# Attention block, v by two levels of block products: the other orientation, two turns, and inner sums kept in DRAM

## The chip, the cores and the metric

The kernel runs on one core of one Trainium2 chip. The metric is the device time of one execution in microseconds (us). Everything is fp32.

## The reference

For 16 images x of 512 channels by 32 x 32 pixels (n = 1024), the block computes group normalisation, one 512 to 1536 projection, attention in 4 heads of 128 channels, an output projection and a residual:

```
xn = (x - mu_group) * rsqrt(var_group + 1e-5) * gamma + beta      # 8 groups
q, k, v = split(qkv_w @ xn + qkv_b)                               # 512 x 1024 each
attn = softmax(q^T k / sqrt(128))                                 # per head, 1024 x 1024
out = x + proj_w @ (attn applied to v) + proj_b
```

## The kernel before

**Layout.** An image is four tiles `x` of 128 channels by 1024 pixels. A head is eight steps. Each step computes scores for 128 keys against two halves of 512 queries (`s`, L609), takes their exponential on ScalarE (`p`, L614), adds `p` into the running denominators `tot` on VectorE (L620, L622), and multiplies the `p` of the step before by v (`po`, L694). The stationary operand of L694 is a block of v laid out as [m, d]: 128 pixels on the partitions, 128 channels of the head in the free dimension.

**Block products.** The projections use seven products in place of eight for a 2 x 2 block product (`strassen`, in the order 1, 2, 6, 5, 7, 4, 3, with two accumulators `x` and `y` in PSUM). A unit is one of the seven products with its eviction: ScalarE copies (`kept_copy`, L399, and L484), VectorE adds (L486, L570). q/k and the output projection use two levels of it (`two_levels`): seven outer products in four groups `OUTER`, each of seven inner ones, so 49 products of 128 x 128 weights with 256 columns in all. For the inner level VectorE makes four sums of the outer operand (`inner_sum`, L460), in single-buffered tiles `in_t1` to `in_t4`. `combine` adds the groups, and `finish` writes the result. q/k is done in two pairs of heads, and both pairs make the same inner sums of the same image. v uses one level only (`v_units`): weights move and x is stationary, so that v comes out as [m, d] directly. That is two times seven products of four 256-column matmuls, 56 per image, evicted by L568 and L570.

**Order.** `plan_head` spreads the units of other stages over the eight steps of each head. For image b: head 0 carries q/k pair 1 of image b, head 1 the projection of image b-1 together with the load and statistics of image b+1, head 2 v of image b+1, head 3 q/k pair 0 of image b+1. Statistics are `bn_stats` and `bn_aggr` on VectorE (L40, L41); normalisation is an activation on ScalarE (L82). The sums of x for the outer level (`x_sums`, L255) stand at the start of head 2. From this program a scheduler makes the order of each engine's instructions, which each engine then follows in turn. DMAs are issued by SP's queue, also in turn: weights from DRAM (L331, v's L541), residual and output (L581, L594), and for the denominators a row written to DRAM and read back broadcast (L641, L643), which the division L704 waits for.

**Buffers.** Two weight tiles (`w`), four tiles of x, three of v, three of `p`, four `y`, two PSUM banks for scores, and two each for `x` and `y`.

Of the kernel before, what the change touches and what calls it, by code (L numbers as in the profile page):

```python
# [27 lines left out]
class Norm:  # L28
# [49 lines left out]
    def apply(self, xn, x, sc, sh, c, on_scalar):  # L78

        i = slice(c, c + 1)  # L80
        if on_scalar:
            self.nc.scalar.activation(xn, x, AF.Identity, bias=sh[:, i], scale=sc[:, i])  # L82
        else:
            self.nc.vector.tensor_scalar(xn, x, sc[:, i], sh[:, i], ALU.mult, ALU.add)
# [69 lines left out]
def fast_path(ctx, tc, x, sources, out, consts, flag, dims):  # L154
# [4 lines left out]

    nc = tc.nc  # L160
# [60 lines left out]
    def stats_chunk(b, c):  # L221
        if c == 0:
            mvs[b] = gn.tile([P, NCC, 2], F32, tag="mv", name=f"mv_{b}")
        norm.chunk(mvs[b], xs[b, c], c)
# [5 lines left out]
    def normalise(b, c, half):  # L230
        t = xs[b, c][:, ts(half, HALF)]
        sc, sh = scaled[b]

        norm.apply(t, t, sc, sh, c, b > 0 or c % 2 == 1)
# [37 lines left out]
    def raw_blocks(site):  # L272


        if site == "proj":
            first, second = proj_wT[:, 0:HC], proj_wT[:, HC:C]
        else:
            first = qkv_wT[:, site * Q : (site + 1) * Q]
            second = qkv_wT[:, C + site * Q : C + (site + 1) * Q]
        return {  # L280
            "a11": first[: C // 2, :], "a12": first[C // 2 :, :],
            "a21": second[: C // 2, :], "a22": second[C // 2 :, :],
        }
# [10 lines left out]
    for site in (*range(PAIRS), "proj"):  # L294
# [4 lines left out]
    store["v"] = kept.tile([P, 7, KC, HC], F32, name="kept_v")  # L299
# [3 lines left out]
    def stage_blocks(site):  # L303
# [4 lines left out]
        if site == "proj":  # L308
# [70 lines left out]
    def v_sums():  # L379
        nc.vector.tensor_sub(wv["s2"], wv["s1"], wv["a11"])  # L380
        nc.vector.tensor_sub(wv["s3"], wv["a11"], wv["a21"])
        nc.vector.tensor_sub(wv["s4"], wv["a12"], wv["s2"])
        for i, p in enumerate(ORDER):
            nc.sync.dma_start(store["v"][:, i], wv[FACTORS[p][0]])
# [50 lines left out]
    def two_levels(name, site, b, blocks, finish):  # L435


        R = {}

# [4 lines left out]
        def group_units(g):  # L444
            group = OUTER[g]
            n = len(group)
            have = {}

            def weights():
                R[g] = rpool.tile([P, 2, 2, HALF], F32, tag=f"r{g % 3}", name=f"{name}_r{g}")  # L450
                have["w"] = group_weights(site, g, b == 0 and site != "proj")

            def inner_sum(m):
                have[m] = tpool.tile([P, 2, Q], F32, tag=f"in_{m}", name=f"{name}_{g}_{m}")
# [4 lines left out]
                for i in range(n):  # L459
                    nc.vector.tensor_sub(have[m][:, i, :], inner(i, a), inner(i, c))  # L460

# [14 lines left out]
            def out_(which, a, c=None):  # L476
# [16 lines left out]
                p5, p7, p4, lambda: (p3(), combine(g)),  # L493
            ]

# [12 lines left out]

        return [group_units(g) for g in range(len(OUTER))]

    def qk_groups(b, pair):
# [14 lines left out]
        return two_levels(f"qk_{b}_{pair}", pair, b, lambda: xb[b], finish)  # L526

    def v_units(b, jj):


        w = {}

        def weights(i):
            if b == 0:
                return wv[FACTORS[i][0]]
            at = ORDER.index(i)
            if at % 3 == 0:
                n = min(3, 7 - at)
                t = wpool.tile([P, 2 * 7 * P], F32, tag="w", name=f"w_v_{b}_{jj}_{at}")
                t = t[:, : n * KC * HC].rearrange("p (i k m) -> p i k m", k=KC, m=HC)  # L540
                nc.sync.dma_start(t, store["v"][:, at : at + n])  # L541
                for j in range(n):
                    w[ORDER[at + j]] = t[:, j]
            return w[i]

        def mm(acc, i, first):
            wi, bn = weights(i), FACTORS[i][1]
# [24 lines left out]
        return strassen(f"v_{b}_{jj}", mm, out_)  # L572

# [115 lines left out]
    def weighted_sum(s, half):  # L689
        b, h, j = where(s)  # L690
        if j == 0 and half == 0:
# [3 lines left out]
            po[b, h][:, i], vs[b, h // 2][:, h % 2, j, :], ps[s][:, i],  # L695
# [29 lines left out]
    def kept_projection():  # L725
        stage_sums("proj")
        for g in range(len(OUTER)):
            group_weights("proj", g, True)
# [106 lines left out]
    def plan_head(b, h):  # L835

        plan = [[] for _ in range(NB)]
        if h == 0:
            spread(plan, staggered(qk_groups(b, 1)), 0, NB)
            if b > 0:  # L840
                plan[3].append(lambda: o_blocks(b - 1))
                plan[3].append(lambda: sums_of_b(ob[b - 1]))
        elif h == 1:
            if b == 0:
                plan[0].append(lambda: stage_blocks("proj"))
                spread(plan, [lambda o=o: bias_of_v(o) for o in range(NCC)], 2, 6)
                plan[6].append(kept_projection)
            else:
                spread(plan, staggered(proj_groups(b - 1)), 0, NB)
            if b + 1 == B:  # L850
                plan[0].append(lambda: last_loads("x"))
            else:
                plan[0].append(lambda: load_x(b + 1))
                spread(plan, [lambda c=c: stats_chunk(b + 1, c) for c in range(NCC)], 2, 6)
                plan[5].append(lambda: stats_group(b + 1))
                plan[6] += [
                    lambda c=c, half=half: normalise(b + 1, c, half)
                    for half in range(NH2) for c in range(NCC)
                ]
# [9 lines left out]
        elif b + 1 < B:  # L869
            if h == 2:  # L870
                plan[0].append(lambda: x_sums(b + 1))
                spread(plan, staggered([v_units(b + 1, jj) for jj in range(2)]), 1, NB)
            else:
                spread(plan, staggered(qk_groups(b + 1, 0)), 0, NB)
# [20 lines left out]
    for half in range(NH2):  # L895
        for c in range(NCC):
            normalise(0, c, half)
    with tc.issue_after(before_power.ins):
        nc.vector.tensor_add(wv["s1"], wv["a21"], wv["a22"])
    v_sums()  # L900
    x_sums(0)
    run(staggered([v_units(0, 0), v_units(0, 1)]))
    stage_sums(0)
    run(staggered(qk_groups(0, 0)))
    stage_blocks(1)
# [3 lines left out]
    for s in range(steps + 1):  # L909
        units = []  # L910
        if s < steps:
# [3 lines left out]
            units = plan[j]  # L915
        if 0 < s < steps and s % NB == 0:
# [146 lines left out]
```

## Time and profile before

| | |
|---|---|
| time, 3 runs | 3233.07 us median (3231.42 to 3233.31) |
| profiled span | 3230.6 us |
| PE busy | 3204.0 us, 99%, 10684 matmul records |
| DVE (VectorE) busy | 2453.7 us, 76% |
| ACT (ScalarE) busy | 1246.6 us, 39% |
| DMA | 357.32 MB, mean 111 GB/s |
| repeat of one image in the chain of waits | 199.2 us |

An fp32 product is two matmul records, and each has a weight load of its own (PEld), which overlaps the matmul before it. A record's duration is longer than the distance to the next one, since matmuls are pipelined; so PE's throughput is read from the distance between starts. A timeline line gives start, duration, engine, source line, operation, output and inputs, and the number of merged records. In the table of windows each line is one stretch of time: its length, then the busy time of PE, PEld, DVE, ACT and POOL, then the granted clock, the DMA share and GB/s.

### The profile page before, as it was taken

To read this page: it belongs to the slowest core of one execution; us is meant where nothing else is said; L and a number is where in the kernel's file an instruction comes from. 1 tells how busy PE (TensorE), PEld (TensorE's weight loads), DVE (VectorE), ACT (ScalarE), POOL (GpSimd) and SP (SyncE) were. 2 spreads that over 40 slices of the span, in tenths; PEclk is the share of its full clock that TensorE was granted. 3 is DMA by queue.
4 is the path that set the end of the run, shared out by engine and by line. 5 is a ranking of instruction groups with operands and counts; after the bars stand their busy time and mean duration, and the time that the engine had idled before them with its cause. 6 is when DMAs were issued, how large, how long until landed. Compare 5 with 4: busy or idle time off the path is not lost.

```text
span 3230.6 us, 31083 instructions
## 1 busy us (share of the span) xinstructions
PE 3204.0 (99%) x10684; PEld 2009.2 (62%) x10684; DVE 2453.7 (76%) x4392; ACT 1246.6 (39%) x2169; POOL 17.6 (1%) x22
## 2 busy tenths in 40 slices
PE   7999999999999999999999999999999999999999
PEld 6566666666666666666666666666666666666654
DVE  7859689586885868868688686877859778596784
ACT  2433334343343333433334333343343334343442
POOL 0000000000000000000000000000000000000000
PEclk9999999999999999999999999999999999999999
DMA  5423333233232333323333333323323333233331
GB/s 171 154 79 126 109 108 125 84 115 120 96 135 74 126 116 104 120 92 116 108 108 120 103 112 109 114 104 107 122 94 115 114 114 117 87 115 109 114 128 40
DMA packets 114837, 357.32 MB, mean 111 GB/s; under 512 B 15472, under 2 KB 27248, under 8 KB 114672
## 3 DMA queue, kind: packets, MB, share of 16 engines
q1 hardware_dynamic: 112800, 353.15, 31.6%
q10 hardware_dynamic: 1872, 2.11, 0.2%
q8 instruction: 86, 1.41, 0.2%
q14 instruction: 79, 0.65, 0.1%
HBM read 308.10 MB, written 47.12 MB: 110 GB/s over the span
## 4 chain that ended last, share of the span: by engine, by line
PE 92%; DVE 6%; ACT 1%; issue 1%; POOL 1%; DMA 0%; SPq 0%; DVEq 0%; POOLq 0%
PE s L609 25%; PE po L694 25%; PE qk_x L471 12%; PE qk_y L471 9%; PE v_x L550 7%; PE v_y L550 5%; PE pp_x L471 5%; PE pp_y L471 4%; DVE tot L622 2%; DVE y L590 1%; DVE y L593 1%; DVE pp_r L503 1%; POOL rstd L64 1%; PE lx L777 0%; DVE pp_r L486 0%
## 5 line engine op out<-in xcount | busy, mean ns | idle before, releaser
L609 PE MATMUL s<-qk,qk 128*128 128x512 f32 x2048 | 1049.0, 594 | 1.8 <-DVE qk L521 1.3
L694 PE MATMUL po<-p,v 128*128 128x512 f32 x2048 | 1045.4, 593 | 0.7 <-ACT p L614 0.7
L614 ACT ACTIVATE p<-s 128x512 f32<-128x512 f32 x1024 | 611.1, 597 | 1065.3 <-PE s L609 1028.1
L622 DVE TENSOR_TENSOR tot<-tot,p 128x1024 f32<-128x1024 f32 x385 | 469.2, 1219 | 313.7 <-ACT p L614 310.7
L694 PEld LDWEIGHTS po<-p,v 128*128 128x128 f32 x2048 | 387.1, 190 | 442.6 <-issue 416.6
L609 PEld LDWEIGHTS s<-qk,qk 128*128 128x128 f32 x2048 | 386.3, 190 | 112.2 <-issue 54.8
L471 PEld LDWEIGHTS qk_x<-qk_t,w 128*128 128x128 f32 x1344 | 250.5, 190 | 200.4 <-issue 139.7
L471 PE MATMUL qk_x<-qk_t,w 128*128 128x256 f32 x1344 | 358.1, 383 | 1.7 <-ACT qk_u L399 1.4
L399 ACT COPY qk_u<-qk_x 128x512 f32<-128x512 f32 (+1 forms) x256 | 136.4, 533 | 238.6 <-PE qk_x L471 238.6
L486 DVE TENSOR_TENSOR qk_r<-qk_y,qk_u 128x512 f32<-128x512 f32 (+1 forms) x256 | 158.7, 620 | 23.5 <-PE qk_y L471 21.2
L550 PE MATMUL v_y<-w_v,x 128*128 128x256 f32 x720 | 173.1, 380 | 0.1
L550 PEld LDWEIGHTS v_x<-w_v,xt 128*128 128x128 f32 x720 | 136.8, 190 | 57.0 <-issue 43.0
L550 PE MATMUL v_x<-w_v,xt 128*128 128x256 f32 x720 | 170.1, 379 | 0.0
L550 PEld LDWEIGHTS v_y<-w_v,x 128*128 128x128 f32 x720 | 135.6, 190 | 55.1 <-issue 40.7
L471 PE MATMUL pp_x<-pp_t,w_proj 128*128 128x256 f32 x630 | 167.8, 383 | 0.0
L471 PEld LDWEIGHTS pp_x<-pp_t,w_proj 128*128 128x128 f32 x630 | 117.2, 190 | 73.7 <-issue 44.5
L471 PE MATMUL qk_y<-x,w 128*128 128x256 f32 x512 | 141.8, 379 | 0.0
L521 DVE SCALAR_TENSOR_TENSOR qk<-qk_r,qkb_sb,qk_r 128x512 f32<-128x512 f32 x192 | 135.5, 746 | 1.5 <-ACT qk_r L484 0.4
L570 DVE TENSOR_TENSOR v<-v_y,v_u 128x512 f32<-128x512 f32 x64 | 43.7, 683 | 116.2 <-ACT v_u L399 71.8
L399 ACT COPY pp_u<-pp_x 128x512 f32<-128x512 f32 (+1 forms) x120 | 63.9, 532 | 161.1 <-PE pp_x L471 150.3
L486 DVE TENSOR_TENSOR qk_r<-qk_y,qk_p 128x512 f32<-128x512 f32 (+1 forms) x128 | 79.2, 618 | 57.3 <-PE qk_y L471 57.3
L471 PEld LDWEIGHTS qk_y<-x,w 128*128 128x128 f32 x512 | 97.3, 190 | 39.7 <-issue 22.0
(174 smaller groups left out, 3445.8 us busy)
## 6 DMA issues: line engine op xcount, KB each, us to landing
w<-kept SPq DMA_DIRECT2D x90, 896.0 KB, 4.5
w_v<-kept_v SPq DMA_DIRECT2D x60, 768.0 KB, 4.2
w_proj<-kept_proj SPq DMA_DIRECT2D x45, 896.0 KB, 4.7
rinv<-row SPq DMA_DIRECT2D x63, 512.0 KB, 3.6
out_y<-y SPq DMA_DIRECT2D x124, 256.0 KB, 2.2
x<-in_x SPq DMA_DIRECT2D x60, 512.0 KB, 4.1
y<-in_x SPq DMA_DIRECT2D x120, 256.0 KB, 3.8
w<-kept SPq DMA_DIRECT2D x30, 448.0 KB, 3.3
```

What stands on the lines that cost most here:

```text
L64: nc.gpsimd.tensor_tensor(rstd, ve, self.neghalf, ALU.pow)
L399: nc.scalar.copy(t[n][:, :width], t["x"][:, :width])
L471: nc.tensor.matmul(acc[:, ts(i, Q)], have["w"][:, i, SLOTS[an], :], inner(i, bn), start=(first and i == 0), stop=True, skip_group_check=True,)
L486: nc.vector.tensor_add(dst, view(a), view(c))
L503: nc.vector.tensor_add(part(2, 0), part(1, 1), part(2, 0))
L521: nc.vector.scalar_tensor_tensor(st[b, h][:, ts(half, HALF)], a[:, r, :], qkb_sb[:, i : i + 1], c[:, r, :], ALU.add, ALU.add,)
L550: nc.tensor.matmul(acc[:, ts(g, HC)], xb[b][bn][k][:, ts(2 * jj + g, P)], wi[:, k, :], start=(first and g == 0 and k == 0), stop=(k == KC ...
L570: nc.vector.tensor_add(dst, view(a), view(c))
L609: nc.tensor.matmul(sc, ks[b, h][:, ts(j, P)], qs[b, h][:, ts(half, HALF)], start=True, stop=True)
L614: nc.scalar.activation(ps[s][:, ts(half, HALF)], sc, AF.Exp, scale=SCALE)
L622: nc.vector.tensor_add(tot[b, h][:, i], tot[b, h][:, i], ps[s][:, i])
L694: nc.tensor.matmul(po[b, h][:, i], vs[b, h // 2][:, h % 2, j, :], ps[s][:, i], start=(j == 0), stop=(j == NB - 1),)
```

## The change

**v.** For images 1 to 15, v goes through `two_levels` like q/k: weights stationary, x moving, 49 products of 256 columns. It comes out as [d, m]. `finish` (in `v_groups`) adds two parts, turns 32 x 32 blocks on VectorE into an interleaved layout, writes 128 x 512 to DRAM (`vd`) and reads it back in four pieces of 32 partitions into v, whose layout is now such that a 128 x 128 block has four floats between neighbouring elements of its free dimension. Image 0 keeps the old v.

**Inner sums.** q/k pair 0 makes the inner sums and also writes them to DRAM (`sums="keep"`); v and q/k pair 1 load them instead of making them (`sums="load"`), each tile one group ahead, the first group's at the last step of the head before.

**Order.** Head 2 now carries q/k pair 0 of the next image and head 3 its v. Statistics of images 1 to 15 move to ScalarE (two passes with an accumulated sum, and three small scalings); normalisation and the sums of x move to steps 5 to 7 of head 1. In image 0, v's weights are combined and kept in head 1, and the first x sums stand after the last VectorE normalisation.

```
-        norm.chunk(mvs[b], xs[b, c], c)
+        if b == 0:
+            norm.chunk(mvs[b], xs[b, c], c)
+            return
+
+        junk = lpool.tile([P, N], F32, tag="tt", name=f"junk_{b}_{c}")
+        sums = gn.tile([P, 3], F32, tag="st", name=f"sums_{b}_{c}")
+        nc.scalar.activation(junk, xs[b, c], AF.Identity, accum_out=sums[:, 0:1])
+        nc.scalar.mul(mvs[b][:, c, 0:1], sums[:, 0:1], 1.0 / N)
+        nc.scalar.mul(sums[:, 1:2], sums[:, 0:1], -1.0 / N)
+        nc.scalar.activation(
+            junk, xs[b, c], AF.Square, bias=sums[:, 1:2], accum_out=sums[:, 2:3]
+        )
+        nc.scalar.mul(mvs[b][:, c, 1:2], sums[:, 2:3], 1.0 / N)
...
+            def sum_tile(h, m):
+                haves[h][m] = tpool.tile(
+                    [P, 2, Q], F32, tag=f"in_{m}", name=f"{name}_{h}_{m}"
+                )
+                return haves[h][m][:, : len(OUTER[h])]
+
+            def load(h, m):
+                if sums == "load" and h < len(OUTER):
+                    nc.sync.dma_start(sum_tile(h, m), inner_kept[b, h, m])
...
+                if sums == "keep":
+                    t = dpool.tile([P, n, Q], F32, tag=f"{m}_{g}", bufs=1, name=f"kept_{m}_{g}")
+                    inner_kept[b, g, m] = t
+                    nc.sync.dma_start(t, have[m][:, :n])
...
-                p5, p7, p4, lambda: (p3(), combine(g)),
+                lambda: (load(g + 1, "t2"), p5()), lambda: (load(g + 1, "t1"), p7()),
+                lambda: (load(g + 1, "t3"), p4()),
+                lambda: (load(g + 1, "t4"), p3(), combine(g)),
...
+    def v_groups(b):
+
+        def finish(which, a, c):
...
+            n = P // BLK
+            for h in range(2):
+                t = ypool.tile([P, HALF], F32, tag="y", name=f"vt_{b}_{pair}_{h}_{half}")
+                nc.vector.tensor_add(t, a[:, h, :], c[:, h, :])
+
+                u = ypool.tile([P, HALF], F32, tag="y", name=f"vu_{b}_{pair}_{h}_{half}")
+                nc.vector.transpose(
+                    u.rearrange("p (q i j) -> p j q i", q=n, i=BLK),
+                    t.rearrange("p (j q i) -> p j q i", q=n, i=BLK),
+                )
+                row = dpool.tile([P, HALF], F32, tag="v", name=f"vd_{b}_{pair}_{h}_{half}")
+                nc.sync.dma_start(row, u)
+                for q in range(n):
+                    nc.sync.dma_start(
+                        vs[b, pair][ts(q, BLK), h, half].rearrange("m (k i) j -> m k (i j)", k=n),
+                        row.rearrange("(k m) (q e) -> q m k e", m=BLK, q=n)[q],
+                    )
...
+    def v_block(b, h, j):
+        v, n = vs[b, h // 2][:, h % 2], NB // NH2
+        return v[:, j, :] if b == 0 else v[:, j // n, :, j % n]
...
-                spread(plan, staggered([v_units(b + 1, jj) for jj in range(2)]), 1, NB)
-            else:
-                spread(plan, staggered(qk_groups(b + 1, 0)), 0, NB)
+        elif h == 2:
+            spread(plan, staggered(qk_groups(b + 1, 0)), 0, NB)
+        else:
+            spread(plan, staggered(next_v.pop()), 0, NB)
```

## The prediction

> **What bounds the kernel now.** I read the page's busy line first, then the costliest groups, then the timeline in a quiet stretch, then the windows of one image.
>
> ```profile
> PE 3204.0 (99%) x10684; PEld 2009.2 (62%) x10684; DVE 2453.7 (76%) x4392; ACT 1246.6 (39%) x2169; POOL 17.6 (1%) x22
> ...
> L609 PE MATMUL s<-qk,qk 128*128 128x512 f32 x2048 | 1049.0, 594 | 1.8 <-DVE qk L521 1.3
> L694 PE MATMUL po<-p,v 128*128 128x512 f32 x2048 | 1045.4, 593 | 0.7 <-ACT p L614 0.7
> ...
> L694 PEld LDWEIGHTS po<-p,v 128*128 128x128 f32 x2048 | 387.1, 190 | 442.6 <-issue 416.6
> ...
> L550 PE MATMUL v_y<-w_v,x 128*128 128x256 f32 x720 | 173.1, 380 | 0.1
> ```
>
> PE is busy 99% of the span and its groups wait for next to nothing. A busy PE need not be at its peak, so the timeline of PE must give the real price of a product (each fp32 product is two records, "x2"):
>
> ```profile
> 575.62 1.02 PE L694 MATMUL po<-p,v 128*128 128x512 f32 x2
> 576.47 1.89 PE L550 MATMUL v_x<-w_v,xt 128*128 128x256 f32 x8
> 578.20 1.02 PE L609 MATMUL s<-qk,qk 128*128 128x512 f32 x2
> 579.06 1.02 PE L694 MATMUL po<-p,v 128*128 128x512 f32 x2
> ```
>
> Start to start, a 512-column product takes 0.858 us (578.20 to 579.06) and four 256-column products 1.73 us, so 0.432 each. One image, from the built order of PE: 64 scores and 64 weighted sums of 512 columns (128 x 0.858 = 109.8), and 203 products of 256 columns (q/k 98, projection 49, v 56; 203 x 0.432 = 87.7): 197.5 us. The chain of waits repeats every 199.2 us (for example "PE po" at 759.00, 958.22, 1157.44). So only 1.7 us per image is not peak matmul, small statistics products included. Columns can be saved, waits hardly.
>
> The second view is the windows of one image; the columns are PE, PEld, DVE, ACT, POOL, then clock and DMA share:
>
> ```profile
> 494.00:504.00 10.00, 10.00 (x33) 5.89 (x31) 10.00 (x19) 4.57 (x9) 0.00 (x0) 1.00 0.43 159
> ...
> 554.00:564.00 10.00, 10.00 (x33) 5.58 (x32) 9.85 (x23) 6.59 (x12) 0.00 (x0) 1.00 0.35 135
> 564.00:574.00 10.00, 10.00 (x36) 6.56 (x35) 6.62 (x12) 2.96 (x5) 0.00 (x0) 1.00 0.22 79
> 574.00:584.00 10.00, 10.00 (x36) 6.54 (x35) 2.15 (x3) 2.96 (x5) 0.00 (x0) 1.00 0.10 26
> ```
>
> DVE is full around the projection and nearly idle in the v stage behind it. That idle time is the reserve from which DVE catches up.
>
> **What the Trainium skill says.** TensorE: Matmul & The Clock Gate, step-by-step part: weights of the next product are loaded under the current one. The trace agrees: the 190 ns load of the weighted sum ends in an "issue" gap of 0.24 us. SBUF — State Buffer, the note on cachelines under Door 1: fp32 reads 16 bytes apart touch a new line each and pay a penalty, without a figure. No row here shows such a load. ScalarE: Activation LUTs, What ACT_TABLE_LOAD costs: 186 ns + 0.833 ns per column, 93 ns more per pointer operand. The trace agrees (L82, two pointers, 512 columns: 799; L763, one pointer, 1024: 1150). DMA: Bandwidth & Descriptors, Two DMAs through the same engine are not ordered: a read of what a DMA wrote must wait for its completion; the row/rinv pair already does (1.3 us, then 3.6 us to landing).
>
> **The change, part by part, per image of 15 (image 0 keeps the old v).**
>
> *PE.* v falls from 56 to 49 products of 256 columns: 7 x 0.432 = 3.02 us, times 15 = 45.4 us. This is the only part that acts directly on the path.
>
> *PE weights.* v now lies in SBUF with 4 floats between neighbours, so each weighted sum loads strided weights. Lower bound 190 ns (no penalty). If reading takes twice as long, 128 columns go from about 107 to 213 ns above the same fixed part: about 297 ns, an estimate from the 190 and the page. Behind a 512-column pass of 429 ns that is hidden; behind a 256-column pass (215 ns) it shows 82 ns. The built order has about 14 such places per image, up from 8: 1.1 us. Upper bound at four times, about 510 ns: 81 ns on both passes of all 64, 10 us. I take 0.5 us.
>
> *DVE.* Removed: 8 bn_stats and 4 aggregates (8 x 0.669 + 4 x 0.197 = 6.1), 28 inner sums of q/k pair 1 now loaded (28 x 0.415 = 11.6), 6 v evictions (6 x 0.682 = 4.1): 21.8 us. Added: 12 evictions at 0.62 (7.4), three 1024-wide combinations at 1.22 (3.7), 8 adds at 0.685 (5.5), 8 transposes of 512. No row shows these: half of L629's 1240 ns plus its fixed part gives 0.70, with strided writes at most double, 1.4; at 0.70 it is 5.6. Sum 22.2. So DVE's total is unchanged (+0.4, up to +6). Only its place changes.
>
> *ACT.* Removed 8 copies at 0.584 (4.7). Added 16 copies at 0.532 (8.5) and the statistics, by the page's price 1.04 + 1.13 + 3 x 0.19 = 2.7 per chunk, 11.0 in all. 78 us becomes 93 of some 197; hidden in sum, but the statistics lie as one block of about 17 us (with exponentials and copies between) in the projection, and DVE's mean copy (L47) waits for its end.
>
> *DMA and SP.* 46 DMAs and 21.7 MB per image become 132 and 36.5 MB: 8 row writes and 32 reads of 64 KB for v, 16 writes and 32 loads of inner sums, 4 instead of 6 v weight loads. Issues at about 0.33 us: 44 us of SP, of 197. 36.5 MB in 197 us is 185 GB/s; the first 20 us of the trace moved 270. SP waits for each row write (1.3 us for 4 KB, 2.2 for the 256 KB of out_y); behind it in the queue stand the first weights of q/k pair 1 and the rinv load. PE's pair-1 products and DVE's division wait for those. In the built order PE has 15 score/weighted-sum pairs (25.7 us) between v's last product and pair 1's first, so this wait is covered; v's own second half is needed about 17 us after its last product against some 12 (eviction 0.7, adds and transposes 2.8, write 2.2, issues 2.6, landing 3 to 4).
>
> *Where it comes back.* The built order pushes pair 1 of q/k into one clump: 49 products with only 8 of 512 columns between, 28.0 us, and then the projection, 47.3 us. DVE work placed there, summed by the rows and scaled by 0.91 (the same sum for the kernel before gives 167.8 us per image where DVE is busy 152.6): 25.2 and 50.2 us. So 75.4 us of DVE stand against 75.3 of PE. In the old order this pair had 95.1 against 98.1. Within the clump each block's c22 eviction (copy 0.53, add 0.62) sits between its p7 and its p3, with 0.86 to 1.7 us of PE work between; at the clump's end the projection's first inner sums queue behind q/k finishes and the denominators. I count 2 us of stall there and 1 us in the projection beyond today's: bounds 0 and 8, as the q/k stage that follows (DVE 35.5 of 49.1) can absorb a lag. But 1.7 of today's total already holds such waits, so I add 1.3 net of them. With the weights: 3.0 - 0.5 - 1.3 = 1.2 us kept per image, 18 us.
>
> *Start and tail.* DVE is full from 60 to 140 us (19.2, 18.2, 19.7, 17.2 of 20). 28 sums leave it, 16 kept writes and the keeping of v's weights (some 11 us of DVE, in head 1, where DVE is busy 5.75 of 20) come: -3 us, between -8 and +4. The last projection is unchanged.
>
> Sum against the profiled span: 3230.6 - 18 - 3 = 3209.6; runs lie 1 to 3 us above that span, so 3211.
>
> **Rivals.** (1) *Full gain*: the order was laid out so that loads and DVE just arrive; 45.4 + 3: about 3185. For it: today only 1.7 us per image is lost although DVE is full in places. (2) *Nothing left*: 3.0 us of stalls per image, 3233. (3) *Slower: DVE becomes the bound from the q/k clump through the projection.* Around the projection DVE was busy about 52 of 57 us, 91%, waiting for PE and ACT in turn; at 91%, 75.4 us take 82.9, which is 7.6 beyond PE, less 3.0 saved and less the part of today's 1.7 that lies there: up to +4 per image, 60 us; half of that absorbed gives 3262. It decides from 3.0 us of added stall, which is DVE at 96% of that stretch. Against it: a full window of 10.00 exists and stalls can be made up later. (4) *Strided weights at a quarter of the rate*: 10 us per image, 150 - 48: about 3335. Against it: a penalty of that size must be in the memory, and the page gives none. (5) *It does not do what it says*: excluded by the built order, which has the 49 products.
>
> **How the numbers follow.** Forecast (1 to 2.5 us kept, 3192 to 3222) 0.42; full gain 0.22; nothing left 0.11; DVE-bound 0.19; strided weights 0.06. Faster 0.42 + 0.22 = 0.64, same 0.11, slower 0.25; 0.2% (6.5 us) is about what a measurement of this kernel can tell from no change. The range leaves out a twentieth below 3182 and, above 3255, the strided weights and the worse part of the DVE case.
>
> **What would show it.** Matmul records about 210 fewer; DVE busy near 2450; weights of po at 190 to 300 ns; PE idle for DVE or ACT in the clump and at the projection's first sums; repeat near 198.0. Wrong if po's weights exceed 430 ns, if PE waits for w or t loads by more than 1 us per image, or if the repeat is over 199.2.

## The result, and the profile after

The changed kernel takes 3281.01 us (median of 4 runs, 3278.69 to 3282.86) against 3232.57 us before: a ratio of 1.015, with a 95% interval of 1.0132 to 1.0167. It is slower by 48 us. The profiled spans are 3281.0 and 3230.6 us.

The busy line and the DMA line of the page, and two of its groups (line, engine, operation, count, then busy us and mean ns of one):

```profile
PE 3203.2 (98%) x10474; PEld 2157.9 (66%) x10474; DVE 2509.4 (76%) x4161; ACT 1444.5 (44%) x2709; POOL 23.1 (1%) x22
...
DMA packets 308600, 589.30 MB, mean 180 GB/s; under 512 B 36800, under 2 KB 137664, under 8 KB 308416
...
L755 PEld LDWEIGHTS po<-p,v 128*128 128x128 f32 x2048 | 597.0, 303 | 320.9 <-issue 190.1
...
L617 DVE STREAM_TRANSPOSE vu<-vt 128x512 f32<-128x512 f32 x120 | 134.8, 1123 | 1.5
```

There are 210 matmul records fewer, as the change says, so 45.4 us of products are gone. PE is busy for almost as long as before all the same. The time came back as idle time, and the view of waits of PE says behind what (us in total, times, longest); the first three rows have no counterpart in the kernel before, whose longest row, "pm" apart, is shown below them:

```profile
PE qk_x L501 <- DMA w<-kept: 16.5, 23, 1.3
PE v_y L501 <- DVE v_r L516: 16.5, 15, 1.1
PE pp_x L501 <- DMA w_proj<-kept_proj: 14.0, 16, 1.7
```

```profile
PE pp_y L471 <- DVE pp_r L486: 2.3, 14, 0.2
```

These rows don't hold all of it, as a matmul that starts late by the time of a weight load is in none. So I also summed, from the timeline of PE, what lies between the starts of two matmul records beyond the 0.429 us (512 columns) or 0.216 us (256 columns) that a record takes at its peak. I call this the stall. It is 39.7 us before and 136.3 us after: 96.6 more, less the 45.4 saved, is 51.2; the spans differ by 50.4. By place, in us per image, in the mean of nine images:

| us after the statistics product "pm", and what the changed kernel does there | before | after | run 11 below |
|---|---|---|---|
| 0 to 20, statistics and the projection's end | 0.9 | 0.7 | 0.7 |
| 20 to 70, q/k pair 0 | 0.1 | 2.9 | 1.5 |
| 70 to 145, v, most of it at its end | 0.2 | 1.9 | 0.3 |
| 145 to 175, the clump of q/k pair 1 | 0.2 | 1.2 | 0.2 |
| 175 on, the projection's first product and after | 0.1 | 1.3 | 0.0 |
| sum | 1.5 | 8.0 | 2.7 |
| repeat of an image | 199.2 | 202.7 | 197.45 |

Run 11, the fastest kernel of the study, shows what of each place can be avoided; at q/k pair 0 it keeps 1.5 us, waits of 0.1 to 0.3 us at ScalarE's copies, VectorE's evictions and weight loads, and so about 1.4 of the 2.9 there can be avoided. Most of that is late weights: in that place of the changed kernel the waits for w alone are 1.4 us per image (0.2 in run 11).

The weights land later than before; the DMA issues of the page (KB each, median us from issue to landing), first those of the kernel before, then those of the changed one:

```profile
w<-kept SPq DMA_DIRECT2D x90, 896.0 KB, 4.5
...
w_proj<-kept_proj SPq DMA_DIRECT2D x45, 896.0 KB, 4.7
```

```profile
w<-kept SPq DMA_DIRECT2D x90, 896.0 KB, 6.3
...
w_proj<-kept_proj SPq DMA_DIRECT2D x45, 896.0 KB, 7.1
```

One projection start, with one of the two longest waits of the fifteen, shows what this does. First the timeline of SP's queue, then that of PE:

```profile
2726.41 0.42 SPq L642 DMA_DIRECT2D y<-in_x  x1
2727.34 0.33 SPq L203 DMA_DIRECT2D x<-in_x  x1
2727.71 0.43 SPq L346 DMA_DIRECT2D w_proj<-kept_proj  x1
```

```profile
2732.94 1.02 PE L670 MATMUL s<-qk,qk 128*128 128x512 f32 x2
2733.79 0.68 PE L501 MATMUL qk_y<-x,w 128*128 128x256 f32 x2
2736.17 1.13 PE L501 MATMUL pp_x<-o,w_proj 128*128 128x256 f32 x4 [1.70 <-DMA w_proj<-kept_proj]
```

The weights are issued at 2727.71, right behind a y and an x load on SP's queue, and land 8.42 us later, among the x, y and inner sums issued around them; from 2726 to 2737 us the queue moves 320 GB/s. PE has 6.6 us of other work in between and then stands. Landing time against the work that lies between issue and first use is the number that decides; I call the latter the slack.

The second wait is at the end of v, in the timelines of DVE and of PE:

```profile
1461.21 0.70 DVE L614 TENSOR_TENSOR vt<-v_r,v_r 128x512 f32<-128x512 f32 x1
1461.81 1.22 DVE L683 TENSOR_TENSOR tot<-tot,p 128x1024 f32<-128x1024 f32 x1
1462.93 1.11 DVE L617 STREAM_TRANSPOSE vu<-vt 128x512 f32<-128x512 f32 x1
1463.85 0.71 DVE L614 TENSOR_TENSOR vt<-v_r,v_r 128x512 f32<-128x512 f32 x1
1464.60 1.12 DVE L617 STREAM_TRANSPOSE vu<-vt 128x512 f32<-128x512 f32 x1
1465.54 0.44 DVE L516 TENSOR_TENSOR v_r<-v_y,v_p 128x256 f32<-128x256 f32 x1
```

```profile
1466.36 0.70 PE L501 MATMUL v_y<-x,w_v 128*128 128x256 f32 x2 [1.12 <-DVE v_r L516]
```

DVE works without a gap from 1455.8; the eviction of v's bank stands behind adds and transposes of the quarters just finished, and v's last product waits for it, in every image.

### The profile page after: what moved, and what is told of

Its sections match the earlier page's. It is cut to its first block, busy times and chain, and to the rows that moved or that the text cites. A ratio compares the mean times of both kernels' runs of the same rounds, so it can differ in the third digit from the quotient of the medians.

```text
span 3281.0 us, 33653 instructions
## 1 busy us (share of the span) xinstructions
PE 3203.2 (98%) x10474; PEld 2157.9 (66%) x10474; DVE 2509.4 (76%) x4161; ACT 1444.5 (44%) x2709; POOL 23.1 (1%) x22
## 3 DMA queue, kind: packets, MB, share of 16 engines
q1 hardware_dynamic: 306544, 584.97, 53.6%
## 5 line engine op out<-in xcount | busy, mean ns | idle before, releaser
L755 PE MATMUL po<-p,v 128*128 128x512 f32 x2048 | 1059.3, 599 | 1.0 <-ACT p L675 0.7
L755 PEld LDWEIGHTS po<-p,v 128*128 128x128 f32 x2048 | 597.0, 303 | 320.9 <-issue 190.1
L501 PE MATMUL qk_x<-qk_t,w 128*128 128x256 f32 x1344 | 367.5, 390 | 2.0 <-ACT qk_u L411 1.7
L501 PEld LDWEIGHTS qk_x<-qk_t,w 128*128 128x128 f32 x1344 | 238.7, 189 | 149.6 <-ACT qk_u L411 81.4
L411 ACT COPY qk_u<-qk_x 128x512 f32<-128x512 f32 (+1 forms) x256 | 136.3, 533 | 269.6 <-PE qk_x L501 267.4
L501 PEld LDWEIGHTS v_x<-v_t,w_v 128*128 128x128 f32 x630 | 118.4, 190 | 79.1 <-issue 38.3
L516 DVE TENSOR_TENSOR v_r<-v_y,v_u 128x512 f32<-128x512 f32 (+1 forms) x120 | 74.9, 624 | 124.5 <-ACT v_u L411 114.1
L501 PE MATMUL v_x<-v_t,w_v 128*128 128x256 f32 x630 | 166.6, 381 | 0.0
L617 DVE STREAM_TRANSPOSE vu<-vt 128x512 f32<-128x512 f32 x120 | 134.8, 1123 | 1.5
L501 PE MATMUL qk_y<-qk_t,w 128*128 128x256 f32 x448 | 122.6, 385 | 1.7 <-DMA qk_t<-kept_t 0.7
L411 ACT COPY v_u<-v_x 128x512 f32<-128x512 f32 (+1 forms) x124 | 66.3, 535 | 123.3 <-PE v_x L501 93.2
```

The lines of the kernel that those rows point to most:

```text
L411: nc.scalar.copy(t[n][:, :width], t["x"][:, :width])
L501: nc.tensor.matmul(acc[:, ts(i, Q)], have["w"][:, i, SLOTS[an], :], inner(i, bn), start=(first and i == 0), stop=True, skip_group_check=True,)
L516: nc.vector.tensor_add(dst, view(a), view(c))
L617: nc.vector.transpose(u.rearrange("p (q i j) -> p j q i", q=n, i=BLK), t.rearrange("p (j q i) -> p j q i", q=n, i=BLK),)
L755: nc.tensor.matmul(po[b, h][:, i], v_block(b, h, j), ps[s][:, i], start=(j == 0), stop=(j == NB - 1),)
```

## The experiments

Three theories stood after the first comparison. Q: v's row DMAs, queued on SP ahead of pair 1's loads, clump q/k pair 1, and the clump costs the time. D: DVE's transposes hold v's last products. T: the traffic makes weights land late. Rival (4), strided weights, was a fourth. Each kernel was timed beside the kernel before; ratios are to that. The median of the kernel before moved between 3230.1 and 3232.6 us from one group of runs to the next, so differences in us between groups are uncertain by about 2 us.

**1. v's DMAs on the POOL queue (theory Q).**

```diff
-                nc.sync.dma_start(row, u)
+                nc.gpsimd.dma_start(row, u)
...
-                    nc.sync.dma_start(
+                    nc.gpsimd.dma_start(
```

> The row writes and reads of v (40 DMAs per image) are issued from POOL's queue instead of SP's, all else the same; the built order then interleaves q/k pair 1 with scores again. Theory Q (queue: v's write-wait-read chain on SP holds up the weights behind it, so pair 1 becomes a clump whose weights, copies and evictions have half the lead): the stall of the clump (1.2 us per image) and most of that at the projection's first product (1.0) go, perhaps 1 more in the weight waits: 2 to 3.5 us per image, 3228 to 3250. Theory T (traffic: 589 MB, weights land in 6.3 us instead of 4.5 wherever they are issued): within 10 us of 3281. Theory D (the strided transposes of 1.12 us at the end of v): within 10 us of 3281 too.

Measured: 3362.31 us, ratio 1.0405 (1.039 to 1.0419). The clump is dissolved in the built order (16 and 16 products of 512 columns between the 49), and the kernel is 81 us slower still. The forecast fails. The stall at the projection does go (1.3 to 0.0 us per image), but that of pair 1 rises from 1.2 to 7.6. DVE's timeline shows the new wait, once per image:

```profile
1508.86 1.23 DVE L681 TENSOR_TENSOR tot<-p,p 128x1024 f32<-128x1024 f32 x1 [1.04 <-ACT p L675]
1516.81 1.23 DVE L765 TENSOR_TENSOR o<-o,rinv 128x1024 f32<-128x1024 f32 x1 [6.73 <-DMA rinv<-row]
```

The rinv load was issued at 1509.47 and landed 7.3 us later, among v's rows, inner sums, x and w. DVE takes its work in order, so q/k's evictions stood behind it, and PE behind them (75.4 us in 15 waits). But this load is not much later than in the changed kernel (6.9 against 6.2 us, in the mean of nine images). What is new is DVE's built order: there 4.4 us of other work lie between the issue of rinv and the division, here almost none, so moving the DMAs also moved the work that covered them. Part of the loss is also a lower clock behind these waits (see run 9). Another queue gives no other engines to move the bytes: the Trainium skill says so (DMA: Bandwidth & Descriptors, Issuing engines are not separate DMA queues), and this run agrees: SP's and POOL's transfers take 47.0 and 6.2% of the time of the 16 engines, and SP's alone took 53.6% before the edit. Theory Q itself fails by runs 4 and 9: both leave v's rows on SP, and pair 1 is no clump in them.

**2. Transposes that write close together (theory D).** This leaves out the interleaved order of v's floats.

```diff
-                    u.rearrange("p (q i j) -> p j q i", q=n, i=BLK),
+                    u.rearrange("p (j q i) -> p j q i", q=n, i=BLK),
```

> The 32x32 transposes write in steps of one element instead of four; v's pixels then stand in the wrong places, so this leaves out the interleave of v's layout; every instruction keeps its place. Theory D: transposes fall from 1.12 to about 0.7 us, the wait of v's last products for the eviction on DVE (1.4 us per image at the end of v) falls by 1 to 1.7, so 3255 to 3266. Theory Q and T: 3275 to 3281.

Measured: 3260.82 us, 1.0095 (1.008 to 1.011), 20 us less than the change. The groups of DVE show why:

```profile
L617 DVE STREAM_TRANSPOSE vu<-vt 128x512 f32<-128x512 f32 x120 | 84.7, 705 | 1.5
```

With 0.42 us less for each of the four transposes ahead of it, the eviction comes in time: the wait at v's end, 1.26 us per image before v_y's product, is 0.0 in this trace, and 15 x 1.26 is 19 us. Theory D holds for that place.

**3. Weights of the weighted sum read close together (rival 4).** This leaves out the right order of v's columns.

```diff
-        return v[:, j, :] if b == 0 else v[:, j // n, :, j % n]
+        if b == 0:
+            return v[:, j, :]
+        flat = v.rearrange("p n d k -> p (n d k)")
+        return flat[:, ts(j, P)]
```

> The weighted sum reads 128 neighbouring floats of v instead of every fourth one; this leaves out v's right order of pixels; every instruction keeps its place. The weight load falls from 303 to 190 ns. Theory S (strided weights cost time wherever a 256-column product precedes, 82 ns each): 1.1 us per image, 3264. What the trace shows instead: no stall behind 256-column products, 0.2 us at each of three first products of a head: 0.6 us per image, 3272. Theories Q, T, D: nothing more than that.

Measured: 3278.57 us, 1.0147 (1.0131 to 1.0162). The weight load falls from 303 to 190 ns, and 2.4 us come back, which the intervals don't tell from none. Strided weights are nearly free here: a load of 303 ns lies under a record of 429.

**4. No inner sums kept or loaded (theory T).** All are made on DVE, as before the change.

```diff
-            f"qk_{b}_{pair}", pair, b, lambda: xb[b], finish, "load" if pair else "keep"
+            f"qk_{b}_{pair}", pair, b, lambda: xb[b], finish, "make"
...
-        return two_levels(f"v_{b}", "v", b, lambda: xb[b], finish, "load")
+        return two_levels(f"v_{b}", "v", b, lambda: xb[b], finish, "make")
...
```

> All inner sums are made on DVE again, in v too; none is written or loaded (16 writes and 32 loads, 11 MB per image less; 56 sums, some 22 us of DVE per image more, DVE then near 175 of 200). Theory T: weights land in 4.5 to 5 us again, 2.5 us of weight waits per image go, but DVE takes back part: 3245 to 3270. Theory Q alone: the clump half stays, since v's chain is still on SP; DVE gets worse: 3285 to 3330.

Measured: 3261.84 us, 1.0092 (1.0076 to 1.0107), 19 us less, although DVE is busy 2790.8 us now. Stalls at q/k pair 0, in the clump and at the projection fall from 5.4 to 2.7 us per image, but those from v on up to pair 1 rise from 1.9 to 3.1, for DVE has more ahead of the evictions. So T looks like a real term, part of whose gain is given back at D's place. The edit also changes the built order, though (pair 1 is no longer a clump, and the projection's slack grows from 6.6 to 9.2 us), so this run alone doesn't separate T from the clump; runs 13 to 17 do better.

**5. Two of v's transposes handed out later (theory D).** The closures of quarter c22 are run one per unit of the last group.

```diff
+                turns.append(turn)
+                if which != "c22":
+                    turns.pop()()
...
```

> The changed kernel, but the two transposes of v's quarter c22 (and their ways through DRAM) are handed out one at a time between the last group's evictions instead of in a row ahead of them; TensorE's order is unchanged to the instruction. Theory D (v's last products wait for an eviction that stands behind a row of 1.12 us transposes on DVE, 1.3 us per image, 20 us in all): most of it comes back, 3260 to 3270. If the 20 us of the contiguous transposes came from DVE's total load instead of from this one place: 3276 to 3284.

Measured: 3282.66 us, 1.0158 (1.0141 to 1.0175): a miss. The order of PE is unchanged; the wait before v's last product only falls from 1.26 to 1.13 us. In the trace one of the two transposes still stands ahead of each of the last evictions, and the backlog, not these two transposes, is what they queue behind. So the run doesn't test its other forecast, that run 2's gain came from DVE's total load. Run 9 does: there four transposes leave this place, DVE's total hardly changes (2524.9 us), and the stall at v's end goes all the same.

**6. The kernel before, with copies that nobody waits for (theory T).**

```diff
+    def copy_beside(tag, n):
...
+        for i in range(n):
+            nc.sync.dma_start(spare[tag][:, i], x[0, ts(i, P), 0 : 2 * P])
...
```

> The kernel before, with copies from DRAM to DRAM added that nobody waits for: 11 MB per image (the changed kernel adds 14.8), issued on SP where the q/k and v products are planned. TensorE's order is unchanged. Theory T (busy DMA engines make weights and rinv land late, and PE waits for them): w lands in 5.5 us or more instead of 4.5, PE waits for w, 3243 to 3262. Rival (order of stages and DVE alone explain the loss, the traffic is harmless): 3230 to 3236.

Measured: 3415.2 us, 1.057 (1.054 to 1.0601), far more than expected. Having nothing to wait for, the copies were issued early and all ran in the first 1190 us. That makes one run its own comparison; the windows (PE, PEld, DVE, ACT, POOL busy, then clock, DMA share and GB/s):

```profile
400.00:800.00 400.00, 351.87 (x1108) 217.38 (x1107) 246.87 (x436) 127.43 (x222) 1.01 (x1) 0.94 0.82 237
1600.00:2000.00 400.00, 399.69 (x1339) 251.91 (x1338) 305.98 (x546) 156.54 (x273) 2.01 (x2) 1.00 0.33 110
```

The same instructions repeat every 222 to 241 us at 237 GB/s, and every 199.21 us at 110. w (896 KB) lands in 6.8 us in the first part and in 4.7 in the second. Transfers that nobody waits for can stop PE. How much of this is landing, how much is SP, which had 1316 more DMAs to issue in its order, and how much the lower clock behind the waits (see run 9), this run doesn't separate.

**7 and 8. A layout with runs of 128 bytes (D), and the same with all sums made (D and T).**

```diff
-                    u.rearrange("p (q i j) -> p j q i", q=n, i=BLK),
+                    u.rearrange("p (q j i) -> p j q i", q=n, i=BLK),
...
+                for k in range(n):
+                    nc.sync.dma_start(
+                        row.rearrange("m q j d -> m (q j) d")[:, :, ts(k, BLK)],
+                        u[ts(k, BLK)].rearrange("m (e i) -> m e i", i=BLK),
+                    )
...
```

> The changed kernel with another layout of v that computes the same: the transposes write runs of 32 floats (128 bytes), the row writes put them in place in DRAM, 4 writes and 4 reads per row tile, and the weights of the weighted sum lie close together. Its order clumps q/k pair 1 as the changed kernel's does. Theory D: L617 near 0.70 us, the wait at v's end gone, 3255 to 3268. If the writes of 128-byte runs load the DMA engines so much that weights land later still: 3275 or more.

> The layout of the run of 128-byte runs, and all inner sums made on VectorE, none kept in or loaded from DRAM. Theories D and T are separate terms of about 20 us each, so they add: 3235 to 3250. If both cured the same wait (at v's end and the q/k start behind it), the second buys little: 3255 to 3262. VectorE carries 3.5 us per image less for the transposes and 23 us more for the sums; if that makes it the bound, 3262 or more.

Measured: 3496.34 us, 1.0819 (1.0801 to 1.0837), and 3407.54 us, 1.0538 (1.0521 to 1.0556). Both miss, by a new wait: "PE po L756 <- DMA v<-vd" 157.4 us in 15 waits, and 128.7 us in the second. Four writes of 64 KB in place of one, each waited for on SP before v can be read, put v's last rows off until the weighted sum waits for them, some ten us per image. Their times say nothing on D; their traces fit it: the transposes take 706 and 702 ns, and the wait of v_y for DVE has no row in either.

**9. v's quarters in the order in which they are needed.** c12 (heads 0 and 1) is finished first; c22 is only added up before it, and c22's transposes and all of c21 (heads 2 and 3) come after.

```diff
-                finish("c21", part(2, 0), part(2, 1))
+                if site != "v":
+                    finish("c21", part(2, 0), part(2, 1))
                 finish("c22", part(2, 0), part(0, 1))
             elif g == 3:
                 finish("c12", part(1, 0), part(3, 0))
+                while site == "v" and turns:
+                    turns.pop(0)()
+                if site == "v":
+                    finish("c21", part(2, 0), part(2, 1))
...
```

> The changed kernel, computing the same, with v's quarters finished in another order: c22 is only added up (its transposes wait), then c12 (heads 0 and 1, needed next) is finished, and c22 and c21 (heads 2 and 3) are turned after it. So four transposes and two adds leave the place ahead of v's last evictions, and the built order no longer clumps q/k pair 1 (48 products with 19 and 18 of 512 columns between, where the changed kernel has 4 and 4). Theory D (DVE's backlog at v's end, 1.3 us per image): at least 20 us come back, 3255 to 3262. If the clump costs what its place shows (1.2 us in it and 1.1 at the projection's first product behind it): up to 30 us more, 3228 to 3254. If late landings alone decide: 3262 to 3280.

Measured: 3281.88 us, 1.0156 (1.0139 to 1.0172): nothing. But not because nothing happened. The stall from v on falls from 1.9 to 0.2 us per image and in pair 1 from 1.2 to 0.2; at the projection it rises from 1.3 to 4.4:

```profile
PE pp_x L501 <- DMA w_proj<-kept_proj: 40.7, 16, 4.2
```

The gain was given back one stage later. The 3.1 us moved and the sum stayed (8.0 and 8.3). Only 2.9 of the 4.4 are the wait itself. Most of the rest is a lower clock behind it: after 8 of the 15 waits PE's granted clock is 0.5 for 3.4 or 6.8 us. Two windows of PE just behind such a wait, the first in the changed kernel (wait 1.9 us), the second here (3.2 us); the number before the last two is the clock:

```profile
2736.20:2743.00 6.80, 6.80 (x24) 4.96 (x25) 6.65 (x21) 4.48 (x10) 0.00 (x0) 1.00 0.58 214
```

```profile
2740.20:2743.60 3.40, 3.40 (x10) 2.69 (x9) 1.85 (x4) 0.69 (x2) 0.00 (x0) 0.50 0.43 125
```

The changed kernel's waits, none over 1.9 us behind its first image, bring no such stretch.

**10. Weights of a group in two DMAs.**

```diff
-            nc.sync.dma_start(w[:, : len(group)], store[site, g])
+            for i in (ds(0, 2), ds(2, 5)):
+                nc.sync.dma_start(w[:, : len(group), i], store[site, g][:, :, i])
```

> The changed kernel, with each load of a group's weights in two DMAs, the two slots that the first two products read and then the other five. No buffer and no byte more. Theory T (late landings of w and w_proj hold PE: 2.8 us per image at the start of q/k pair 0, 1.1 at the projection's first product): the first part lands in 3 to 4 us instead of 6 to 8, and 25 to 38 us come back, 3243 to 3257. If PE only waits there for other reasons (VectorE's evictions, the order on SP): 3274 to 3284.

Measured: 3279.9 us, 1.0154 (1.0137 to 1.0171): a miss again. The stall of q/k pair 0 falls from 2.9 to 1.5 us, as expected, but pair 1 rises from 1.2 to 1.8, v's end stays at 1.9, and only 1.0 us of 8.0 goes in the trace, which is of the fastest of four executions. At the projection the first part lands in 4.1 us instead of 7.5, but in this built order only 3.7 us of work lie between its issue and its use, where there were 6.6.

**11 and 12. Urgent order and all sums made; the same with weights in two.** Edits 9 and 4, then also 10.

> The order of quarters of the run urgent first, and all inner sums made on VectorE, none kept in or loaded from DRAM; the built order has 16 products of 512 columns of each kind between the 49 of every stage. Terms D and T and the clump are then all removed: what is left of the 6.4 us per image is the start of q/k pair 0 (about 1 us) and strided weights (0.6), 3215 to 3235. If VectorE, which carries 23 us per image more, takes over: 3250 or more.

> The run before (urgent quarters first, sums made), with the weights of a group in two DMAs as well. If weights still land too late at the starts of stages: another 8 to 20 us off that run, 3200 to 3222. If the smaller traffic alone already lets them land in time: within 4 us of it.

Measured: 3207.72 us, 0.9931 (0.9914 to 0.9948), and 3212.84 us, 0.9943 (0.9926 to 0.9959). The first is the fastest kernel of this study and beats both. Its waits hold no row of weights over 1.6 us, and its busy line shows that DVE at 87% is no bound:

```profile
PE qk_y L501 <- DVE qk_r L516: 1.9, 3, 1.0
PE s L684 <- ACT p L689: 1.8, 1, 1.8
PE qk_y L501 <- DVE pp_r L516: 1.7, 11, 0.2
PE qk_x L501 <- DMA w<-kept: 1.6, 5, 0.4
```

```profile
PE 3174.0 (99%) x10474; PEld 2176.0 (68%) x10474; DVE 2797.9 (87%) x5029; ACT 1439.0 (45%) x2709; POOL 23.1 (1%) x22
```

An image repeats every 197.45 us with 2.7 us of stall. Where weights land in 4.5 to 4.7 us anyway, splitting them buys nothing and costs 5 us.

**13 to 15. Which part of the keeping costs the 74 us between runs 9 and 11.** On run 11, only the writes of pair 0's sums ("keep", "make", "make" for q/k pair 0, q/k pair 1 and v); then v's loads with them; then pair 1's loads with them.

> The run urgent order with all sums made, plus the 16 writes of the inner sums of q/k pair 0 per image to DRAM, which nothing reads; the order of TensorE's products is the same but for some 30 lines. The writes stand in the stage of q/k pair 0, where w landed late in the changed kernel. If they are what makes w late there (2.8 us per image in that stage): 3225 to 3245. If writes are harmless: 3205 to 3212.

> The run before with v's inner sums loaded from DRAM too; q/k pair 1 still makes its own. Same order of products. In the changed kernel nothing in v's stage waited for a load (PE's waits name w and w_proj alone), so the loads for v are cheap: within 6 us of the run with the writes alone. If bytes in all set the cost: a third of 74 us, some 25 more than the writes alone.

> The run with the writes alone, with q/k pair 1's inner sums loaded from DRAM, v's made. Its order of products is that of the run with the urgent order alone (19 and 18 of 512 columns in pair 1's stage). Theory T in its narrow form (pair 1's loads run together with x, y and the projection's weights, w_proj lands in 8 us and PE waits 2.9 us per image for it): most of the 74 us comes back, 3250 to 3285. If bytes in all set the cost: 3225 to 3245.

Measured: 3223.84 us, 0.9976 (0.9967 to 0.9986); 3225.62 us, 0.9979 (0.9971 to 0.9988); 3290.64 us, 1.0179 (1.0162 to 1.0196). The writes cost 16 us, nearly all of it where pair 0's weights land (stall 1.5 to 2.6 us there). v's loads cost 2, which the intervals don't tell from none. Pair 1's loads cost 67, up to 19 of them by the lower clock behind the waits (half of 37.5 us at clock 0.5), though runs 14 and 15 move nearly the same number of bytes (530.56 and 534.22 MB). So it is not the bytes of the whole span, it is the place: pair 1's loads meet those of x, y and the projection's weights. The three costs add up to 85 us and not to 74: run 15, whose TensorE order is run 9's, is 9 us slower than it, which stays unexplained. The projection's first product, in means over the images; "moved" is what all DMAs moved from the issue of its weights to their landing:

| kernel | landing, us | moved, MB | slack, us | stall, us |
|---|---|---|---|---|
| before | 4.7 | 1.2 | 11.5 | 0.0 |
| after | 7.5 | 2.4 | 6.6 | 1.0 |
| 9, urgent order | 8.6 | 2.3 | 5.8 | 2.9 |
| 10, weights in two (first part) | 4.1 | 1.2 | 3.7 | 0.5 |
| 11, run 9 and sums made | 4.5 | 1.1 | 11.4 | 0.0 |
| 14, and writes and v's loads | 4.6 | 1.2 | 11.4 | 0.0 |
| 15, or writes and pair 1's loads | 8.9 | 2.4 | 5.8 | 3.2 |
| 17, run 9 with weights in two (first part) | 3.7 | 0.9 | 3.8 | 0.1 |

Landing less slack gives the stall to 0.1 us in each row where it is positive. With pair 1's loads both change: the load takes longer, and the built order leaves less work between its issue and its use. In the changed kernel and in runs 9 and 15, either the landing or the slack of the kernel before would have been enough. The rate in GB/s while the load is under way doesn't tell the kernels apart (265 before and 265 in run 15); the bytes that move beside it do.

**16. Statistics of x back on DVE**, on run 11.

```diff
-        if b == 0:
+        if True:
             norm.chunk(mvs[b], xs[b, c], c)
             return
```

> The run urgent order with all sums made (3207.7), with the statistics of x back on VectorE as in the kernel before (12 instructions, 6 us per image there, ScalarE freed of some 11 us per image). If ScalarE's block of statistics holds no one up and VectorE is not full: 3205 to 3211. If VectorE, busy 83 to 85% by then, becomes the bound around the projection: 3215 to 3235.

Measured: 3231.39 us, 0.9996 (0.9987 to 1.0004). The move to ScalarE is worth 24 us (21 by the ratios) once the sums are made on DVE, which is busy 89% here. The new wait is for q/k evictions that come late from DVE (1.9 us in run 11):

```profile
PE qk_y L501 <- DVE qk_r L516: 16.7, 16, 1.6
```

**17. Urgent order and weights in two, all sums kept and loaded as in the change.** Edits 9 and 10.

> The run with the urgent order (3281.9), each load of a group's weights in two DMAs, the first with the two slots that the first two products read. Traffic is the same. If the landing of the first weights is what holds PE at the projection (2.9 us per image) and at the start of q/k pair 0 (2.8): the first part lands in 4 to 5 us and 40 to 70 us come back, 3212 to 3242. If the burst only passes the wait on to the second part or to the next load in the queue: 3265 to 3284.

Measured: 3222.84 us, 0.9973 (0.9966 to 0.9979). This run joins the two terms. It moves as much as the changed kernel (589.34 MB) and is 58 us faster, while its two edits gave nothing one at a time (3281.9 and 3279.9). The first part of the weights lands in 3.7 us, and of the 40.7 us of run 9's wait 5.5 are left:

```profile
PE pp_x L502 <- DMA w_proj<-kept_proj: 5.5, 8, 1.8
```

Its built order is near that of run 9 (17 and 16 products of 512 columns in pair 1's stage), and its slack even shorter. So with this slack it was the late landing, not a lack of bandwidth in the mean, that stopped PE at the projection, and D's place and T's places stand in one line: what one lets through, the next holds.

## Why the prediction was wrong

**What was right.** 210 records and 45.4 us of products less. Strided weights: 303 ns against an estimated 297. Their cost was near the 0.5 us taken, but by luck: behind the 256-column products, where it was counted, the trace shows no stall, and 0.6 us per image come at three weighted sums that follow another one (0.25 in run 3). DMA: 180 GB/s against 185. ACT: 13.2 us more per image ((1444.5 - 1246.6)/15) against 15, and hidden. v's rows land in time: in the changed kernel the weight loads of the weighted sum wait for them 0.2 us at most, and PE not at all.

**The step that failed first: "DMA and SP".** It worked out the mean rate and checked one chain of transfers, v's rows, against the work that covers it. It left w and w_proj at their old landing times and did not set them against the work that covers them. At the projection's start the landing went from 4.7 to 7.5 us and that work from 11.5 to 6.6. They were on the path: about 1.4 us per image at q/k pair 0 and 1.3 at the projection, by the comparison with run 11, and so 2.7 of the 6.4 us added (96.6/15), the largest single term. The other terms are 1.6 at v's end, 1.0 in the clump and 1.4 of small waits in q/k pair 0, which now lies right behind the projection (in sum 6.7, less 0.2 saved behind "pm"). The page gave 4.7 us for w_proj, and the built order gives the slack and the loads that stand beside it. The prediction named the case itself, "if PE waits for w or t loads by more than 1 us per image": the waits name 30.5 us for w and w_proj, 2.0 per image, and 0.7 in the whole span for a t load.

**The second: "That idle time is the reserve from which DVE catches up".** It was argued from sums of whole stages. At v's end it is a matter of 10 us: DVE was full from 1455.8 to 1466, with four transposes in it, and each took 1.12 us where the prediction took 0.70 (its upper bound was 1.4). That term is 1.26 to 1.6 us per image, from a place where the prediction counted none. In the sum, DVE's total rose by 55.7 us, 3.7 per image, against a forecast of +0.4 up to +6; eight transposes at 0.42 more are 3.4 of it.

**"Where it comes back".** The clump and the projection were right places to look. Counted were 2 and 1 us more than before; measured are 1.0 and 1.2. In the clump half of the stall, 0.6 of 1.2 us, stands behind weight loads that waited for ScalarE's copies, which is the kind of wait that was named. At the projection the cause was wrong: of the 1.3 us none is left where the weights land early (run 11), so it isn't inner sums queued behind finishes. Then the sum went wrong. The 3 us were counted as beyond today's, and 1.7 of today's were subtracted from them once more; today's stall lies elsewhere, most of it at the projection's end (0.9, and 0.7 after the change), and stays. Without that step the sum gives -0.5 us per image kept, about 3237. But most of what came, 4.5 us per image, came at q/k pair 0 and at v's end, where the prediction counted nothing. Rival (3), DVE as the bound in that stretch, fails: run 11 gives DVE 19 us per image more and is the fastest. There is little room above that, as run 16 shows. Rivals (2) and (4) fail by the sum and by run 3. Rival (1), the full gain, is what the products are worth, but no run reached it; run 11 keeps 22 of the 48 us (against the 3230.1 measured beside it).

**The range.** The stall of "bounds 0 and 8" included what came, 6.4 us more per image, though it was set for the clump and the projection alone. The upper end of the range, 3255, did not use that bound; with it, 3231 + 15 x (8.0 - 3.0) would have been about 3306.

**What stays open.** How the loads for pair 1 divide between a later landing and a shorter slack, as the built order changes with them; why run 5's transposes moved so little in DVE's order; and what holds the other half of the clump's stall.

## What to carry to other kernels

For each load that the bound engine needs, compare its landing time in the traffic of that very stretch with the work that the built order puts between its issue and its first use, and count the bytes that are queued beside it: the mean rate of the span, here 180 GB/s, told nothing, and even the rate while the load was under way was 265 GB/s both in the kernel before, with a landing of 4.7 us, and in run 15, with 8.9. An edit of one wait can change the built order and with it such a slack (runs 1, 4 and 10), so read the slack again after each. Finish first what is needed first, and keep work for later heads out of the way of evictions. Where several waits stand in one line, an edit that removes one alone can measure as nothing: two such edits gave nothing here (within 1 us), and 58 us together.

## What the runs showed of the hardware that was not expected

- A transpose of 128x512 fp32 in blocks of 32x32 takes 705 ns when it writes runs of floats and 1123 ns when its writes lie 16 bytes apart.
- A load of 128x128 fp32 weights takes 190 ns, and 303 ns from floats 16 bytes apart.
- 896 KB of weights land in 4.5 to 4.7 us where 1.1 to 1.2 MB move until then, their own included, and in 7.5 to 8.9 us where 2.3 to 2.4 MB do.
- A DMA issued from POOL occupies it for 0.55 us (0.33 to 0.43 on SP). v's row writes and reads land in 4.3 us when POOL issues them (run 1), and in 2.1 and 2.2 when SP does (medians).
- A longer wait of PE costs more than its length. In the traces of all kernels here, start and end left out, none of 296 waits of 1 to 2 us (stalls as counted above) was followed by a lower granted clock, 32 of 56 of 2 to 4 us were, and all 55 longer ones. The clock is then 0.5 for 3.4 us or a small multiple of it, and no such stretch stands without a wait of over 2 us ahead of it. In run 6 these stretches make up the 0.94 of its loaded part; in run 1 they are 99 us.
- An activation with an accumulated sum is followed on ScalarE by a read of the accumulator, an instruction of its own of 186 to 191 ns. The prediction's 2.7 us per chunk of statistics left that out; the instructions of one chunk sum up to 3.2.
